# ScalarE in a written-out order beside TensorE, in the three attention stages of a two-layer decoder

## The chip, the cores and the metric

The kernel runs on one core of one Trainium2 chip, in one launch. The metric is the device time of that core in microseconds. It is built with a tile framework: the program says which engine runs each operation, the framework adds the semaphores, places the buffers of each named pool, and puts each engine's instructions in order. Inside a block called a manual schedule, the engines that are named keep the order in which the program states their operations; all others are ordered by the framework's planner, which uses costs of its own.

PE is TensorE, DVE is VectorE, ACT is ScalarE, POOL is GpSimd and SP is SyncE, whose queue issues most of the loads.

## The reference, cut to what matters

The input x has 16 sequences of 112 rows of 512 values. Two layers follow each other, each with a self attention, a cross attention and a feed-forward part:

```python
x = x + _L0_attn_ref(_layernorm(x), qkv, proj)       # 16 heads of 32, over the sequence axis
x = x + _L0_xattn_ref(_layernorm(x), ctx, ...)       # fp8-rounded inputs; self and cross attention
x = x + _L0_ffn_ref(_layernorm(x), ...)              # mixture of 8 experts
x = x + _L1_attn_ref(_layernorm(x), ...)             # 16 heads of 32, causal
x = x + _L1_xattn_ref(_layernorm(x), ctx, ...)
x = x + _L1_ffn_ref(_layernorm(x), ...)              # ternary weights
```

The change touches three of these: the two attentions with 16 heads of 32, and the self attention of the fp8 part:

```python
# _L0_attn_ref and _L1_attn_ref, per sequence and head
scores = q @ k.T * scale            # causal mask
probs  = softmax(scores)
out    = (probs @ v) @ w_proj.T

# _L0_xattn_ref, self part
ln  = _ln(x, ln_w, ln_b)
xq  = fp8(bf16(clip(ln / in_scale)))          # four scales: q, k, v and the cross part's q
q   = _ln(xq @ wq.T); k = _ln(xq @ wk.T); v = xq @ wv.T      # 16 and 8 heads of 128
core = softmax(q @ k.T / sqrt(128)) @ v
out  = fp8(core / smooth) @ wproj.T           # the self half of the projection
```

## The kernel before

The program runs seven stages in a row, each with its own buffers. Three of them put PE's order down by hand, in a manual schedule for PE alone.

**The two narrow attentions** (`stage_attn0`, `stage_attn1`, both through `narrow_attention`). The work is cut into quads: one quad is one group of 128 rows (first attention, 14 quads in blocks of 2, 4, 4, 2 and 2) or one sequence of 112 rows (second attention, 16 quads in blocks of 4), with 16 heads as four quarters of four heads. `NarrowQuad` has its steps:

- `scores`: four mask products (L168) and 16 score products in fp32 (L175) into one PSUM tile of four banks, of which there is one. Then, for each quarter, DVE takes the row maximum (L182) and scales it (L183), ACT takes four exponentials with their sums (L187), DVE the reciprocal (L191), and POOL multiplies (L192).
- `transpose_probs`: PE transposes a quarter's probabilities (L199) into the single buffer `tr`, and ACT copies it to SBUF (`ptt`, L201).
- `values`: PE multiplies with the values (`ps_av`, L208), and after the last quarter DVE copies the result (L213).

While quad n's scores are made, quad n-1 is transposed and multiplied quarter by quarter, quad n-2 gets its output product (`after`: `ps_o`, L273, and the sum onto x), and between the quarters the next block is prepared (`before`): the normalized input is transposed (`NormedRows.transpose`, L117, also through `tr`, with ACT's copy L149), the queries and keys are made as long products of four matmuls over 512, 448 or 256 columns (`wide`, L310 and L1199), and the values (L319, or L273). Each step carries a cost, and the loop spreads the steps over the quarters by it:

```python
for r in range(4):
    if n:
        made[n - 1].transpose_probs(r)
    while todo and used + todo[0][0] / 2 < budget * (r + 1) / 4:
        cost, step = todo.pop(0)
        used += cost
        step()
    if r == 1 and n > 1:
        quads[n - 2][0].after(quads[n - 2][1])
    if n:
        made[n - 1].values(r)
```

The first attention also gets the weights of the next stage ready (`Weights.part`): SP loads 512 columns, ACT scales them (L493), DVE takes the mean of each head away where the part is centred (L478 to L480), ACT writes the rounded half (L497) and POOL the rest (L498). Twelve such parts are asked for at once, as block 2 is prepared.

**The fp8 self attention** (`stage_fp8_self`). The four head groups of the 16 sequences are 64 units, and `turn(n)` works on five of them at once: unit n is projected (`ps_q` and `ps_kv`, L510, with the squares L589 and L591, the norm by POOL L408 and L409, the products L595 and the copy of v, L599), unit n-1 is transposed and scaled (L608, L400), unit n-2 gets scores and exponentials (L616, L622 to L625, L630), unit n-3 is transposed (L636, L638) and multiplied with its values (L644), then rounded to fp8 (`smooth_fp8`: L657, L421 to L426, whose result is `r_o`), and unit n-4 gets its output product (`ps_acc`, L510, added at L670). For the first head group a turn also takes the inputs of unit n+2: PE transposes them (L117), ACT scales them in 16 instructions (L538), and DVE and POOL round them. Turns also ask for two or three parts of coming weights.

The PSUM tags hold: `mm` two buffers in the narrow attentions and three in the fp8 stage, `tr` one, `sc` four, and in the narrow attentions four banks of scores and one of values.

Of the kernel before, what the change touches and what calls it, by code (L numbers as in the profile page):

```python
# [9 lines left out]
F32 = mybir.dt.float32  # L10
# [118 lines left out]
class NormedRows:  # L129
# [16 lines left out]
    def transpose(self, i):  # L146
        t = self.t
        ps = transposed(self.k, self.xn[i], t)
        self.k.nc.scalar.copy(self.xt[:, :, i * t : (i + 1) * t], ps)  # L149
        if i + 2 < len(self.rows):  # L150
            self.normalize(i + 2)


class NarrowQuad:
# [9 lines left out]
    def scores(self):  # L164
# [14 lines left out]
        self.pr = []  # L179
        for r in range(4):  # L180
            mx = k.small.tile([t, 4], F32, tag="nq_m", name="nq_m", bufs=6)
            nc.vector.tensor_reduce(mx, ps[:, :, r * t : (r + 1) * t], AX.X, ALU.max)  # L182
            nc.vector.tensor_scalar(mx, mx, -self.scale, None, ALU.mult)  # L183
            sums = k.small.tile([t, 4], F32, tag="nq_s", name="nq_s")
            pr = wk.tile([t, 4, t], F32, tag="pr", name="pr", bufs=8)
            for j in range(4):
                nc.scalar.activation(  # L187
                    pr[:, j, :], ps[:, j, r * t : (r + 1) * t], AF.Exp, bias=mx[:, j : j + 1],
                    scale=self.scale, accum_out=sums[:, j : j + 1],
                )  # L190
            nc.vector.reciprocal(sums, sums)  # L191
            nc.gpsimd.tensor_tensor(pr, pr, bc(sums.unsqueeze(2), [t, 4, t]), ALU.mult)  # L192
            self.pr.append(pr)
# [22 lines left out]
def narrow_attention(k, blocks):  # L216
# [5 lines left out]
    with k.tc.manual_schedule(engines={mybir.EngineType.PE}):  # L222
# [3 lines left out]
        for n in range(len(quads) + 1):  # L226
            budget = 0.0
            if n < len(quads):
# [4 lines left out]
                budget = sum(cost for cost, _ in todo) / (block.groups - group)  # L233
                made.append(block.quad(group))
                made[n].scores()
            used = 0.0
            for r in range(4):
                if n:
                    made[n - 1].transpose_probs(r)
                while todo and used + todo[0][0] / 2 < budget * (r + 1) / 4:  # L240
                    cost, step = todo.pop(0)
                    used += cost
                    step()
                if r == 1 and n > 1:
                    quads[n - 2][0].after(quads[n - 2][1])
                if n:
                    made[n - 1].values(r)
            while n < len(quads) and todo and group == block.groups - 1:
                todo.pop(0)[1]()
        block, group = quads[-1]  # L250
        block.after(group)
# [27 lines left out]
class Attn0Block:  # L279
# [13 lines left out]
    def before(self):  # L293
# [13 lines left out]
        def wide(dst, w):  # L307
            ps = k.psum.tile([P, 512], F32, tag="mm", name="ps_q", bufs=2)
            for c in range(KC):
                nc.tensor.matmul(ps[:, :n], w[:, c], xt[:, c, :n], start=c == 0, stop=c == 3)  # L310
            nc.vector.tensor_copy(dst, ps[:, :n])

        def queries(g):
# [1266 lines left out]
```

## Time and profile before

| | |
|---|---|
| median of 3 runs | 4186.39 us (4182.59, 4191.33, 4186.39) |
| profiled execution | 4182.83 us |
| its span | 4181.1 us |
| instructions | 47902 |
| PE busy | 3821.5 us, 91% |
| DVE busy | 1857.1 us, 44% |
| ACT busy | 1480.5 us, 35% |
| POOL busy | 946.0 us, 23% |
| mean granted clock of TensorE | 0.954 |

The span runs from the first to the last instruction; the execution's own time is 1.7 us longer. PE and PEld are the matmuls and the weight loads of TensorE. A group of the profile is named by its line, engine, operation and tiles, out first; a wait is named by the waiting instruction and by what ended its wait. Shares are averages over seven stages that differ, so stretches of the span are read one by one.

### The profile page before, as it was taken

Reading aid. Unit: us, or ns where it says so; the run is one execution under the profiler, and the core shown is the slowest. Engines: PE = TensorE matmul, PEld = TensorE weight load, DVE = VectorE, ACT = ScalarE, POOL = GpSimd, SP = SyncE. Lnnn points to the kernel's source line nnn. Section 1 sums busy time; section 2 is a strip of 40 time slices with the busy share of each in tenths; the row PEclk is TensorE's granted clock in tenths of the full one; section 3 lists DMA queues with packets and bytes.
Section 4 is the critical chain, followed back from the end, with each engine's and each line's share of the span. In section 5 each row is a group of like instructions: output and inputs, shape, how many; then the busy total and the mean of one; then the engine's idle time right before and its main releaser. Section 6 shows DMA issues by size and latency. Waiting matters only on the chain.

```text
span 4181.1 us, 47902 instructions
## 1 busy us (share of the span) xinstructions
PE 3821.5 (91%) x17118; PEld 2451.9 (59%) x17118; DVE 1857.1 (44%) x4310; ACT 1480.5 (35%) x4185; POOL 946.0 (23%) x1253
## 2 busy tenths in 40 slices
PE   6875887989999999999999999999988989999999
PEld 4444676777566566656666665444434445556887
DVE  4445666675544544554445533111243444214333
ACT  4446656554433433343333321111123341111222
POOL 3224445553322322232222210000122120000000
PEclk8987999999999999999999989999988989999999
DMA  2213212331211211111121113888830004112000
GB/s 84 54 46 120 84 71 99 120 124 69 76 49 48 76 41 48 58 54 48 48 76 46 48 34 124 290 297 295 286 129 11 1 1 130 68 59 90 10 9 18
DMA packets 99759, 359.95 MB, mean 86 GB/s; under 512 B 11952, under 2 KB 26288, under 8 KB 89936
## 3 DMA queue, kind: packets, MB, share of 16 engines
q1 hardware_dynamic: 86784, 327.47, 24.0%
q0 software_dynamic: 5360, 16.52, 1.1%
q10 hardware_dynamic: 7376, 12.89, 0.8%
q8 instruction: 135, 2.21, 0.2%
q14 instruction: 104, 0.85, 0.1%
HBM read 316.47 MB, written 40.37 MB: 85 GB/s over the span
## 4 chain that ended last, share of the span: by engine, by line
PE 70%; DVE 5%; ACT 3%; POOL 2%; DMA 2%; issue 1%; ACTq 0%; SPq 0%; DVEq 0%; POOLq 0%
PE ps_kv L788 14%; PE ps_o L273 5%; PE ps L1104 5%; PE ps_acc L510 4%; PE ps_s L815 3%; PE ps_av L838 3%; PE ps_q L510 3%; PE ps_y L1124 3%; PE ps_o L1391 3%; PE ps_pt L828 3%; PE ps_u L1409 3%; PE ps_q L1199 3%; PE ps_g L1409 2%; PE ps_p L1260 2%; PE ps L1076 2%; PE ps_o L1086 1%
## 5 line engine op out<-in xcount | busy, mean ns | idle before, releaser
L788 PE MATMUL ps_kv<-w_kv,ct 128*125 128x512 f32 x1536 | 690.1, 592 | 0.0
L788 PEld LDWEIGHTS ps_kv<-w_kv,ct 128*125 128x125 f32 x1536 | 287.6, 187 | 319.1 <-issue 278.8
L426 POOL TENSOR_TENSOR r_o<-r_t,r_m 128x448 fp32r<-128x448 bf16 x128 | 133.6, 1044 | 570.5 <-DVE r_t L425 538.8
L1104 PE MATMUL ps<-w_expert,xgt 128*128 128x448 f32 x560 | 219.6, 545 | 31.5 <-ACT xgt L1099 31.5
L409 POOL TENSOR_TENSOR cu_v<-cu_v,mhalf 125x2 f32<-125x2 f32 (+1 forms) x256 | 198.9, 777 | 21.2
L187 ACT ACTIVATE pr<-ps_s,nq_m 112x112 f32<-112x112 f32 (+1 forms) x480 | 166.3, 360 | 100.8 <-DVE nq_m L183 99.6
L192 POOL TENSOR_TENSOR pr<-pr,nq_s 112x448 f32<-112x448 f32 (+1 forms) x120 | 117.9, 982 | 367.7 <-DVE nq_s L191 341.3
L769 DVE TENSOR_REDUCE cu_v<-sq 125x2 f32<-125x256 f32 (+1 forms) x256 | 124.4, 486 | 163.2 <-ACT sq L768 163.2
L408 POOL TENSOR_SCALAR cu_v<-cu_v 125x2 f32<-125x2 f32 (+1 forms) x256 | 49.4, 193 | 650.4 <-DVE cu_v L769 641.2
L815 PE MATMUL ps_s<-kt,qt 128*112 128x375 f32 x512 | 184.0, 480 | 4.8 <-ACT pr L748 4.7
L1104 PEld LDWEIGHTS ps<-w_expert,xgt 128*128 128x128 f32 x560 | 103.6, 190 | 131.3 <-issue 87.7
L746 DVE TENSOR_REDUCE ex_m<-ps_s 112x1 f32<-112x375 f32 (+1 forms) x272 | 148.5, 546 | 62.3 <-PE ps_s L1284 60.2
L768 ACT ACTIVATE sq<-ps_kv 125x256 f32<-125x256 f32 x192 | 73.5, 383 | 268.7 <-PE ps_kv L788 222.2
L400 ACT ACTIVATE qt<-ps_t,vec 128x448 f32<-128x448 f32 x128 | 95.1, 743 | 207.1 <-PE ps_t L799 206.5
L748 ACT ACTIVATE pr<-ps_s,ex_m 112x375 f32<-112x375 f32 (+1 forms) x272 | 155.8, 582 | 28.3 <-DVE ex_m L747 28.3
L792 ACT COPY vn<-ps_kv 125x256 f32<-125x256 f32 x192 | 71.5, 372 | 264.6 <-DVE kn L771 264.6
L838 PE MATMUL ps_av<-pt,vn 125*128 125x224 f32 x768 | 158.7, 357 | 1.1 <-ACT pt L831 1.1
L510 PE MATMUL ps_acc<-w_cross,r_o 128*112 128x512 f32 x512 | 153.4, 422 | 3.2 <-POOL r_o L426 3.2
L838 PEld LDWEIGHTS ps_av<-pt,vn 125*128 125x128 f32 x768 | 147.1, 192 | 8.1 <-ACT pt L831 1.3
L815 PEld LDWEIGHTS ps_s<-kt,qt 128*112 128x112 f32 x512 | 89.5, 177 | 105.9 <-issue 45.7
L828 PEld LDWEIGHTS ps_pt<-ident,pr 112*125 112x125 f32 x768 | 107.8, 190 | 72.5 <-issue 29.0
L510 PE MATMUL ps_q<-w_cross,xq 128*112 128x512 f32 x512 | 150.1, 414 | 0.0
(279 smaller groups left out, 7726.3 us busy)
## 6 DMA issues: line engine op xcount, KB each, us to landing
w_expert<-in_moe_w SPq DMA_DIRECT2D x70, 896.0 KB
ct<-in_ctx_t SPq DMA_DIRECT2D x80, 750.0 KB
w_expert<-in_moe_w SPq DMA_DIRECT2D x35, 1024.0 KB
xq<-xq_dram SPq DMA_DIRECT2D x48, 672.0 KB
xq<-xx_dram SPq DMA_DIRECT2D x64, 224.0 KB
raw<-in_self_w SPq DMA_DIRECT2D x48, 256.0 KB
w_sum<-in_ffn_w SPq DMA_DIRECT2D x12, 1024.0 KB
cn<-in_ctx SPq DMA_DIRECT2D x16, 750.0 KB
```

The lines of the kernel that those rows point to most:

```text
L187: nc.scalar.activation(pr[:, j, :], ps[:, j, r * t : (r + 1) * t], AF.Exp, bias=mx[:, j : j + 1], scale=self.scale, accum_out=sums[:, j : ...
L273: k.nc.tensor.matmul(po, at[:, c, i * t : (i + 1) * t], w[:, c, :], start=c == 0, stop=c == nk - 1)
L409: nc.gpsimd.tensor_tensor(dst, dst, bc(k.minus_half[: dst.shape[0]], [dst.shape[0], n]), ALU.pow)
L510: k.nc.tensor.matmul(out, lhs(c), w[i][:, c, :], start=first and c == 0 and i == 0, stop=last and c == n - 1 and i == 1,)
L746: nc.vector.tensor_reduce(mx, src, AX.X, ALU.max)
L748: nc.scalar.activation(dst, src, AF.Exp, bias=mx, scale=scale, accum_out=sums)
L788: nc.tensor.matmul(pkv, self.ct[:, c, ch * CC : (ch + 1) * CC], w[:, c, :], start=c == 0, stop=c == 3)
L815: nc.tensor.matmul(ps, self.qt[:, h, :], self.kt[:, h // 2, :], start=True, stop=True)
L828: nc.tensor.transpose(ps[:, h, :], self.pr[:, h, ch * CC : (ch + 1) * CC], k.ident[:S, :S])
L838: nc.tensor.matmul(av[:, 2 * g : 2 * g + 2, :], self.vn[:, ch, g, :], self.pt[:, ch, 2 * g : 2 * g + 2, :], start=ch == 0, stop=ch == NCH - 1,
L1104: nc.tensor.matmul(pp, xt[:, c, :], w[:, c, :], start=c == 0, stop=c == 3)
L1409: nc.tensor.matmul(pp, w[:, c, cols], xt[:, part, c, :], start=c == 0 and part == 0, stop=c == 3 and part == 1,)
```

## The change

ACT joins PE in both manual schedules, so its instructions stand in the order of the program too. The program's order is changed to suit:

- In `NarrowQuad`, `scores` keeps the maxima of all four quarters, and the exponentials of a quarter become a step of their own, called after the copy of the same quarter of the quad before.
- The copy of the transposed input (L149) goes from ACT to DVE, in all three users of `NormedRows`: both narrow attentions and the cross attention of the second layer.
- Long products and output products are two steps of two matmuls each (`halves_of`); the steps of `after` stand in the middle of a quad's list.
- The parts of the next stage's weights are asked for one at a time, at the end of each quad (`aside`).
- In the fp8 stage the input's transposes open the turn, its 16 scalings are done as 5, 5 and 6, the projection is split in two with the squares behind each half and v's copy ahead of the norm, the exponentials follow the last scalings, and the values come last in the turn, after the output product.

```diff
-        self.k.nc.scalar.copy(self.xt[:, :, i * t : (i + 1) * t], ps)
+        self.k.nc.vector.tensor_copy(self.xt[:, :, i * t : (i + 1) * t], ps)
...
-        self.pr = []
+        self.ps, self.mx, self.pr = ps, [], []
         for r in range(4):
-            mx = k.small.tile([t, 4], F32, tag="nq_m", name="nq_m", bufs=6)
+            mx = k.small.tile([t, 4], F32, tag="nq_m", name="nq_m", bufs=8)
             nc.vector.tensor_reduce(mx, ps[:, :, r * t : (r + 1) * t], AX.X, ALU.max)
             nc.vector.tensor_scalar(mx, mx, -self.scale, None, ALU.mult)
...
+            self.mx.append(mx)
+
+    def exponentials(self, r):
...
+        for j in range(4):
+            nc.scalar.activation(
+                pr[:, j, :], self.ps[:, j, r * t : (r + 1) * t], AF.Exp,
+                bias=self.mx[r][:, j : j + 1], scale=self.scale, accum_out=sums[:, j : j + 1],
+            )
+        nc.vector.reciprocal(sums, sums)
+        nc.gpsimd.tensor_tensor(pr, pr, bc(sums.unsqueeze(2), [t, 4, t]), ALU.mult)
+        self.pr.append(pr)
...
+def halves_of(k, shape, tag, name, product, then):
+    got = []
+
+    def step(half):
+        if half == 0:
+            got.append(k.psum.tile(shape, F32, tag=tag, name=name, bufs=k.banks[tag]))
+        for c in range(half * KC // 2, (half + 1) * KC // 2):
+            product(got[0], c)
+        if half:
+            then(got[0])
+
+    return [lambda half=half: step(half) for half in range(2)]
...
-    with k.tc.manual_schedule(engines={mybir.EngineType.PE}):
+    with k.tc.manual_schedule(engines={mybir.EngineType.PE, mybir.EngineType.Activation}):
...
+            if n > 1:
+                after = quads[n - 2][0].after(quads[n - 2][1])
+                now[len(now) // 2 : len(now) // 2] = after
+            total, used = sum(cost for cost, _ in now), 0.0
             for r in range(4):
                 if n:
                     made[n - 1].transpose_probs(r)
-                while todo and used + todo[0][0] / 2 < budget * (r + 1) / 4:
-                    cost, step = todo.pop(0)
-                    used += cost
-                    step()
-                if r == 1 and n > 1:
-                    quads[n - 2][0].after(quads[n - 2][1])
+                if n <= last:
+                    made[n].exponentials(r)
+                while now and used + now[0][0] / 2 < total * (r + 1) / 4 + 1.0:
+                    used += now[0][0]
+                    now.pop(0)[1]()
                 if n:
                     made[n - 1].values(r)
...
+            if aside:
+                aside()
...
-        steps = blocks[2].before
-        blocks[2].before = lambda: k.next_w[0].step(12) and steps()
-        narrow_attention(k, blocks)
+        narrow_attention(k, blocks, lambda: k.next_w[0].step(1))
...
         def turn(n):
+            new = inputs.get(n + 2)
+            if new:
+                new.transpose()
+                new.scale(5)
             if at(n):
-                units[n].project(weights[order[n][0]], xq.pop(n))
+                units[n].project_q(weights[order[n][0]], xq.pop(n))
+            if new:
+                new.scale(5)
+            if at(n):
+                units[n].project_kv()
             if at(n - 3):
                 units[n - 3].transpose_probs()
             if at(n - 1):
                 units[n - 1].transpose()
+            if at(n - 2):
+                units[n - 2].scores()
+            if new:
+                new.scale(6)
+            if at(n - 2):
+                units[n - 2].exponentials()
+            if at(n - 4):
+                units[n - 4].output()
             if at(n - 3):
                 units[n - 3].values()
-            if at(n - 2):
-                units[n - 2].scores()
-            if at(n - 4):
-                units[n - 4].output()
-            if n + 2 in inputs:
-                inputs[n + 2].scaled()
-                xq[n + 2] = inputs[n + 2].rounded()
+            if new:
+                xq[n + 2] = new.rounded()
...
-        with k.tc.manual_schedule(engines={mybir.EngineType.PE}):
+        with k.tc.manual_schedule(engines={mybir.EngineType.PE, mybir.EngineType.Activation}):
             for n in range(-2, total):
                 turn(n)
```

## The prediction, made before the changed kernel ran

> **What bounds the kernel now.** I read the busy time by stage first, because the change touches three stages of seven: the first attention (0 to 335 us), the fp8 self attention (335 to 1045) and the second narrow attention (3095 to 3475). The columns are stretch and length, then busy us and instruction count of PE, PEld, DVE, ACT and POOL, the granted clock, and DMA.
>
> ```profile
> 0.00:335.00 335.00, 247.47 (x1656) 143.22 (x1656) 145.70 (x331) 140.60 (x561) 89.96 (x116) 0.85 0.23 63
> 335.00:1045.00 710.00, 587.93 (x3512) 498.77 (x3512) 471.69 (x1100) 411.91 (x1252) 343.20 (x348) 0.93 0.29 99
> 3095.00:3475.00 380.00, 331.92 (x1934) 166.26 (x1934) 145.54 (x330) 133.11 (x596) 84.57 (x89) 0.89 0.03 9
> ```
>
> PE is idle for 88, 122 and 48 us there, 258 of the 360 us that it is idle in the span, and its clock is granted at 0.85 to 0.93. No other engine is full: ACT has 42%, 58% and 35%. So order, not work, is the limit. Second, the waits (waiting instruction, releaser: us, times, longest), first attention and then fp8 stage:
>
> ```profile
> PE ps_av L208 <- ACT ptt L201: 35.9, 28, 4.6
> PE ps_xt L117 <- ACT xt L149: 14.8, 8, 5.9
> ```
> ```profile
> ACT v L599 <- DVE qk L595: 115.7, 58, 4.2
> PE ps_av L644 <- ACT pt L638: 49.4, 21, 4.0
> PE ps_pt L636 <- POOL pr L630: 40.1, 26, 3.4
> ```
>
> PE waits for copies that stand in ACT's queue behind something else. Third, the timeline of one turn of the first attention says behind what:
>
> ```profile
> 209.73 0.37 ACT L187 ACTIVATE pr<-ps_s,nq_m 128x128 f32<-128x128 f32 x1 [1.04 <-DVE nq_m L183]
> ...
> 211.27 0.18 DVE L191 RECIPROCAL nq_s<-nq_s 128x4 f32<-128x4 f32 x1 [1.31 <-ACT pr L187]
> 211.37 0.66 DVE L182 TENSOR_REDUCE nq_m<-ps_s 128x4 f32<-128x512 f32 x1
> ...
> 212.06 0.60 DVE L183 TENSOR_SCALAR nq_m<-nq_m 128x4 f32<-128x4 f32 x1
> ...
> 212.75 0.37 ACT L187 ACTIVATE pr<-ps_s,nq_m 128x128 f32<-128x128 f32 x1 [1.51 <-DVE nq_m L183]
> ...
> 214.13 0.59 ACT L201 COPY ptt<-ps_pt 128x512 f32<-128x512 f32 x1
> ...
> 214.78 0.66 PE L208 MATMUL ps_av<-ptt,vn 128*32 128x128 f32 x8 [4.56 <-ACT ptt L201]
> ```
>
> The reader is to see a loop between two engines: exponentials, reciprocal, next maximum, next exponentials. It turns in 3.02 us (209.73 to 212.75), of which ACT works 1.4, and three groups of exponentials pass before the copy that PE wants. In the fp8 stage 16 scalings are one block ahead of such a copy:
>
> ```profile
> 626.80 5.49 ACT L538 ACTIVATE y<-ps_xt,q_bias,q_gain 128x112 bf16<-128x112 f32 x16
> ...
> 633.53 1.02 PE L644 MATMUL ps_av<-pt,v 112*128 112x224 f32 x4 [2.72 <-ACT pt L638]
> ```
>
> **What the Trainium skill says.** "TensorE: Matmul & The Clock Gate", Part 1, says the array clock is throttled by default and released after about 3.4 us of sustained work. The trace agrees: eight matmuls of ps_o (L273) take 3.60 us between busy neighbours and 6.10 at 94.47, after waits. So a wait removed pays again in clock. "GPSIMD Engine Reference", section 8, says GpSimd shares its SBUF interfaces with VectorE. It fits L183, which takes 0.15 to 0.17 us alone and 0.60 while the 1.04 us product L192 runs on POOL. "Perfetto Trace Analysis", Sequencer Loop, describes an engine's instructions read in turn, each waiting for its semaphores; the 115.7 us that ACT stands before v (L599) is such a queue blocked at its head.
>
> **Part by part: the two attentions.** No arithmetic is added. In the built order of the changed kernel DVE takes the four maxima of a quad right after the scores, and ACT's order is copy, four exponentials, copy, and so on. The loop of 3.02 us becomes ACT's own work: copy 0.59 and exponentials 1.38 (206.72 to 208.10), 1.97 per quarter. A quad with nothing else on PE is then scores 2.07 (106.98 to 109.05), about 1.6 to the first maximum and its scaling, 4 x 1.97: 11.5, with handoffs 12 us. Any other quad is set by PE. Its pieces, start to start at full clock: scores 2.07; per quarter transposes 0.50 and values 0.36; a long product of 512 columns 3.43 to 3.53, of 256 columns 1.73; a value product 0.92; an input transpose 0.50. Halving the long products adds no matmul; it lets copy and exponentials pass beside each half of 1.75.
>
> What is late next is the input transposes: their copy goes from ACT to DVE (no row shows it; the like-sized copy L213 takes 0.69 against 0.59 on ACT), behind four maxima, through a single buffer. I add 6 us for every four transposes, 3 for two; it could be 2 to 10.
>
> First attention, against the starts of the mask matmuls (L168). Quads 2 to 5 take 86.9 now (78.95 to 165.80); PE needs 4 x (2.07 + 3.44 + 3.53) = 36.2, preparation 4 x 0.50 + 5 x 3.43 + 4 x 0.92 = 22.8, and 6: 65, so -22. Quads 6 to 9: 69.4 now; 36.2 + 11.5 + 3 = 51, -19. Quads 10 and 11: 38.4; 18.1 + 11.5 + 3 = 33, -6. Quads 12 and 13: 29.9; 24, -6. Quads 0 and 1: 53.3; 19.5 + 18 = 37.5, -16. Sum **-69**. The weights' loads move from one burst to one part after each quad: 12 loads on SP, 24 instructions on ACT and 6 centerings on DVE. On ACT a centred part is 0.72, some 1.9 for DVE (0.68 + 0.16 + 0.69 of L478 to L480, and handoffs) and 0.62; it lies after a quad's last exponentials, beside 2.07 of scores and 1.6 of maximum, so I cost it nothing. Without that cover it is 3.2 x 6 = 19 us. On SP they queue ahead of loads and stores that have a quad of slack.
>
> Second attention, scores 1.88, quarters 0.76: a block of four quads needs 4 x (1.88 + 3.04 + 3.53) + 1.7 + 24.8 + 14.1 = 74.4, with transposes 80. It takes 87.0 and 86.4 now (3218.09, 3305.11, 3391.48): -6.6, -6. The first four save 6 likewise. The last four have no preparation: 4 x 12 = 48 against 64.5, -16.5. Sum **-35**.
>
> I take three quarters of both, since each floor leaves out handoffs and DVE's order: -52 and -26.
>
> **The fp8 stage.** A turn of PE alone is 8.41 us (951.27 to 1010.14, equal turns). While inputs are scaled, turns average 11.3 (432.48 to 647.73, 19 turns). The change splits the 16 scalings into 5, 5 and 6, puts v's copy ahead of the qk product, so the 115.7 us of blocked ACT go, and puts the values last in the turn. Their copy then has 3.8 us in front of PE's use (0.74 + 0.95 + 2.08 of transposes, scores and output). The store of y follows the last scalings as before; an input's load has one turn ahead of its first use, not nearly two, against 2.9 to 5.9 us that the chain of waits shows for loads of r_y in this stage. ACT's sum in a turn with an input is 5.49 + 0.6 + 0.4 + 0.4 + 0.5 + 0.7 + 0.5 + 1.4 = 10.0, in one without 4.5; a pair is 14.5 against PE's 17.3, so it fits. I put the pair at 18.8: 19 turns save 36, of which I take 27. Against it: the transposes of input 2 now stand ahead of the first projection, which waits for a second block of 5.5 us: +5. And ACT waits in its order for each centring of weights, which the old order filled with other work: 22 centred parts at about 2 us, in turns with 3.6 us of free ACT. I count +12. Without any cover it is +44. Net **-10** (from -31 to +40).
>
> Elsewhere the copy L149 moves to DVE in the stage after (16 x 0.6 us), beside a PE that is busy 341 of 350 us (3470 to 3820): nothing, or 10 us if DVE is late. Untouched stages I leave at zero, within 5 either way.
>
> **The sum.** -52 - 26 - 10 = -88. The profiled execution takes 4182.83 (span 4181.1), so 4094.8; the median of the three runs is 3.56 above it: **4098 us**.
>
> **Rivals.** *A, the order of ACT eats the fp8 part.* For it: 22 centrings without cover and a DVE at 66% in that stage. Against it: the free 3.6 us. The fp8 stage then loses 25 instead of gaining 10: 4186 - 78 + 25 = 4133. *B, slower: the values at the end of the turn make the output wait.* Now a value product has some 10 us until the output reads its rounded result. Afterwards it is 5.9 (projections 3.8, transposes and scores 2.1). In DVE's built order the rounding stands behind the reciprocal, so behind the exponentials; in a turn with an input these end about 2.0 after the values, then 0.3 + 1.84 on DVE + 1.05 on POOL (L426) + 0.3: 5.5. The margin is 0.4. From there every us that ACT is late is a us of PE, in 64 turns; at 1.7 us late it is +109 and the sum +31: 4217. Against it: half the turns have no input, with 2 us more margin. *C, the quads stay paced:* exponentials now also wait for PE's transposes; if a quarter still takes 3 us, only the last quads and some fp8 turns gain, and the result is within 8 us: 4180.
>
> **How the numbers follow.** Forecast 0.71, A 0.15, B 0.10, C 0.04 (about half of C's width counted as no change). Faster by over 0.2%, which is 8.4 us and about what a measurement of this kernel can tell from no change: 0.86; within it 0.04; slower 0.10. Low end: all of the floors and a fp8 stage of -31, so 4186 - 135 = 4051; high end: half of the attentions' floors and +30, so 4164. Range 4050 to 4165.
>
> **What would show it.** Right: in the attentions the wait of PE ps_av for ptt near zero, exponential groups evenly 2 to 4 us apart, clock above 0.92; first attention near 283 us, second near 354. In the fp8 stage L538 in groups of 5 and 6, no wait of ACT v for qk, ps_av waiting little. Wrong: a new wait of PE ps_acc for POOL r_o (B), ACT w_self waiting for DVE raw for over 40 us (A), or quads with no preparation still above 15 us (C).

## The result, and the profile after

The changed kernel takes **4146.44 us** (median of 4 runs, 4141.81 to 4151.72), against 4185.09 for the kernel before (4 runs): a ratio of 0.9906, 95% interval 0.9889 to 0.9923. The change gains 39 us where 88 were forecast. The profiled execution has a span of 4142.4 us and a mean granted clock of 0.959. Below, "before" and "after" are the two kernels of this case.

The busy time by stage of after, in the same columns as before: the first attention, the fp8 self attention and the second narrow attention.

```profile
0.00:292.00 292.00, 229.15 (x1660) 131.75 (x1660) 136.38 (x346) 133.53 (x557) 91.23 (x116) 0.92 0.29 75
292.00:1030.00 738.00, 579.30 (x3513) 495.41 (x3514) 489.56 (x1101) 400.45 (x1243) 346.04 (x348) 0.91 0.29 94
3088.00:3440.00 352.00, 321.08 (x1932) 159.05 (x1932) 139.92 (x347) 122.63 (x577) 81.15 (x86) 0.94 0.05 14
```

In the two attentions PE's idle time is down and its clock is up, 0.85 to 0.92 and 0.89 to 0.94. In the fp8 stage the work is the same, the stretch is longer, and the clock has fallen from 0.93 to 0.91. Three points in the timelines measure this. The first fp8 projection starts at 301.69 us, not 344.81: **-43.1**. From it to the first cross projection the stage takes 729.8 us, not 702.2: **+27.6**. The second attention, from its first input transposes to the next stage's first projection, takes 353.6 us, not 381.7: **-28.1**. The stages that the change hardly touches make up the remaining +4.9.

The waits of after in the fp8 stage (waiting instruction, releaser: us, times, longest) name the new holder. The first attention's old wait comes last:

```profile
PE ps_acc L544 <- ACT pt L692: 64.5, 18, 10.6
ACT w_self L531 <- DVE raw L514: 45.2, 18, 5.1
PE ps_acc L544 <- POOL r_o L460: 13.7, 24, 3.3
ACT w_cross L531 <- DVE raw L514: 15.4, 4, 6.8
```
```profile
PE ps_av L212 <- ACT ptt L205: 7.5, 8, 1.6
```

ACT's wait before v is gone from the list, and PE's wait for ptt has fallen from 35.9 to 7.5 us. In their place ACT waits 60.6 us for the centring of weight parts (45.2 + 15.4), and PE waits 64.5 us for pt at its output product. The timeline of one turn shows how the first makes the second:

```profile
581.26 0.36 ACT L679 ACTIVATE pr<-ps_s,su_m 112x112 f32<-112x112 f32 x1
581.58 0.73 ACT L527 ACTIVATE raw<-raw,w_cols 128x512 f32<-128x512 f32 x1
...
583.27 0.55 PE L690 MATMUL ps_pt<-ident,pr 112*112 112x112 f32 x4
...
584.22 0.62 ACT L531 CAST w_self<-raw 128x512 fp32r<-128x512 f32 x1 [1.91 <-DVE raw L514]
...
584.75 0.72 ACT L527 ACTIVATE raw<-raw,w_cols 128x512 f32<-128x512 f32 x1
...
587.98 0.62 ACT L531 CAST w_self<-raw 128x512 fp32r<-128x512 f32 x1 [2.51 <-DVE raw L514]
...
589.94 0.72 ACT L527 ACTIVATE raw<-raw,w_cols 128x512 f32<-128x512 f32 x1 [1.34 <-POOL w_self L532]
...
592.46 0.62 ACT L531 CAST w_self<-raw 128x512 fp32r<-128x512 f32 x1 [1.80 <-DVE raw L514]
592.99 0.59 ACT L619 ACTIVATE sq<-ps_q 112x512 f32<-112x512 f32 x1
...
593.99 0.56 ACT L692 COPY pt<-ps_pt 112x448 f32<-112x448 f32 x1
...
594.69 3.72 PE L544 MATMUL ps_acc<-w_self,r_o 128*112 128x512 f32 x8 [9.51 <-ACT pt L692]
```

The probabilities are transposed at 583.27, some 0.6 us of PE work. Their copy pt is written behind three weight parts. Each part is a scaling, a wait for DVE, and a cast; the third scaling also waits until a raw buffer is free and loaded, because there are two. So the copy comes at 593.99, and PE, which needs its PSUM bank, stands for 9.51 us.

### The profile page after: what moved, and what is told of

It reads as the page before. It is cut to its first block, busy times and chain, and to the rows that moved or that the text cites. A ratio compares the mean times of both kernels' runs of the same rounds, so it can differ in the third digit from the quotient of the medians.

```text
span 4142.4 us, 47854 instructions
## 1 busy us (share of the span) xinstructions
PE 3783.4 (91%) x17118; PEld 2434.7 (59%) x17118; DVE 1866.1 (45%) x4356; ACT 1445.5 (35%) x4139; POOL 950.3 (23%) x1253
## 4 chain that ended last, share of the span: by engine, by line
PE 70%; DVE 9%; ACT 4%; POOL 4%; issue 2%; DMA 2%; ACTq 0%; POOLq 0%; DVEq 0%
PE ps_kv L853 15%; PE ps L1169 5%; PE ps_acc L544 4%; PE ps_s L880 4%; PE ps_av L903 3%; PE ps_q L544 3%; PE ps_y L1189 3%; PE ps_o L1476 3%; PE ps_o L303 3%; PE ps_pt L893 3%; PE ps_u L1494 3%; PE ps_q L1263 2%; PE ps_g L1494 2%; PE ps_p L1345 2%; PE ps L1141 2%
## 5 line engine op out<-in xcount | busy, mean ns | idle before, releaser
L853 PEld LDWEIGHTS ps_kv<-w_kv,ct 128*125 128x125 f32 x1536 | 287.8, 187 | 318.8 <-issue 278.7
L460 POOL TENSOR_TENSOR r_o<-r_t,r_m 128x448 fp32r<-128x448 bf16 x128 | 134.1, 1048 | 448.7 <-DVE r_t L459 395.0
L544 PE MATMUL ps_acc<-w_self,r_o 128*112 128x512 f32 x512 | 153.2, 447 | 81.9 <-ACT pt L692 64.5
L544 PEld LDWEIGHTS ps_acc<-w_self,r_o 128*112 128x112 f32 x512 | 95.6, 198 | 116.5 <-POOL w_self L532 40.1
L857 ACT COPY vn<-ps_kv 125x256 f32<-125x256 f32 x192 | 71.5, 372 | 264.8 <-DVE kn L836 264.8
L836 DVE TENSOR_TENSOR kn<-ps_kv,cu_v 125x256 f32<-125x256 f32 x192 | 81.6, 425 | 153.9 <-POOL cu_v L443 153.9
```

The source lines that it names most:

```text
L460: nc.gpsimd.tensor_tensor(dst, t, m, ALU.subtract)
L544: k.nc.tensor.matmul(out, lhs(c), w[i][:, c, :], start=first and c == 0 and i == 0, stop=last and c == n - 1 and i == 1,)
L853: nc.tensor.matmul(pkv, self.ct[:, c, ch * CC : (ch + 1) * CC], w[:, c, :], start=c == 0, stop=c == 3)
```

## The experiments

In all of them the fp8 stage is measured from first to first: unit n's projection starts turn n. The turns up to 23 take in the inputs of the first head group; turns 0 to 5 get ready the weight parts of group 1, turns 26 to 38 get ready most of the weight parts of groups 2 and 3; turns 36 to 51 also quantise the cross inputs (`quantize_cross`); turns 48 to 54 get the parts of the cross stage. The column "stage" runs from the first projection to the first cross projection, so it holds turn 63 and the end of the stage too. All times are us, read from the timelines, one profiled execution each. A ratio compares with runs of before from the same session; in brackets is its 95% interval. Eight kernels of this document have the fp8 program of new_pe_vals: their stages measure 661.4 to 671.0, and their single columns agree within 2.1.

| kernel | 0-8 | 8-26 | 26-38 | 38-48 | 48-54 | 54-63 | stage |
|---|---|---|---|---|---|---|---|
| before | 103.0 | 199.9 | 129.1 | 93.5 | 64.1 | 75.7 | 702.2 |
| after | 101.0 | 176.7 | 150.5 | 104.9 | 78.5 | 76.7 | 729.8 |
| attn_only | 102.2 | 203.2 | 131.1 | 90.5 | 65.1 | 75.5 | 704.5 |
| new_pe | 88.7 | 177.1 | 134.8 | 104.3 | 70.7 | 77.3 | 690.8 |
| nocenter | 86.9 | 176.8 | 134.5 | 105.3 | 71.5 | 76.8 | 689.8 |
| spread | 98.2 | 176.7 | 132.9 | 105.1 | 75.9 | 76.3 | 703.6 |
| noround | 101.1 | 176.6 | 150.5 | 86.9 | 70.4 | 76.7 | 702.3 |
| new_pe_vals | 88.2 | 179.1 | 130.4 | 91.0 | 64.4 | 76.9 | 669.5 |
| fixed_vals | 106.2 | 175.7 | 164.1 | 90.9 | 77.1 | 77.0 | 728.4 |
| inputs_last | 100.2 | 206.6 | 130.4 | 90.2 | 64.0 | 76.9 | 706.7 |
| best_spread | 89.2 | 177.2 | 130.7 | 88.4 | 67.8 | 76.9 | 669.7 |

### Order held by whom: ScalarE, or the turn

The first question is which half of the stage's change costs: that ACT is fixed, or that the turn has a new order. Two edits, alone and together, make three kernels beside after.

**attn_only**: `Quantized`, `SelfUnit` and `stage_fp8_self` as before, so the fp8 part of the diff above is undone line by line.

> The two narrow attentions as after, the fp8 self stage as before (its turn order, ScalarE left to the scheduler). Theory (the whole loss is in the fp8 stage, and the stages don't act on each other): first self projection to first cross projection back from 729.8 to about 702 us, total 4146 - 28 = 4118 us. Rival (part of the loss comes from what the new attention hands on: weight parts of group 0 spread over the quads, a later DMA tail): the stage stays above 712 us and the total above 4128.

Measured: 4116.17 us, ratio 0.983 (0.9814 to 0.9846); stage 704.5. The loss lies in the fp8 stage: with that stage's program as before, the attentions keep their gain and the stage is back at before's time.

**new_pe**:

```diff
-        with k.tc.manual_schedule(engines={mybir.EngineType.PE, mybir.EngineType.Activation}):
+        with k.tc.manual_schedule(engines={mybir.EngineType.PE}):
             for n in range(-2, total):
                 turn(n)
```

> The kernel after, with ScalarE of the fp8 stage left to the scheduler; the turn's new order stays, for TensorE. Theory (the fixed ScalarE order costs in the weights and the quantising turns): turns 26-38, 38-48 and 48-54 go back to about 129, 94 and 64 us, and turns 8-26 keep part of their gain, stage 680 to 705 us, total 4097 to 4121. Rival (the turn's order costs): those turns stay at 150, 105 and 78 us, total about 4146.

Measured: 4109.62 us, ratio 0.9817 (0.9801 to 0.9834); stage 690.8. The theory holds for the weights turns (150.5 to 134.8, 78.5 to 70.7) and turns 0-8 (101.0 to 88.7), and falls for turns 38-48, which stay at 104.3: they aren't long because ACT is fixed.

**old_act**: attn_only, with the same line the other way:

```diff
-        with k.tc.manual_schedule(engines={mybir.EngineType.PE}):
+        with k.tc.manual_schedule(engines={mybir.EngineType.PE, mybir.EngineType.Activation}):
             for n in range(-2, total):
                 turn(n)        # before's turn
```

> As the kernel attn_only, but ScalarE too follows the written order in the fp8 stage, with the turn's order of before (projection whole, maxima and exponentials together, the 16 scalings at the turn's end, values ahead of scores). Theory (a fixed ScalarE order is what costs): the weights turns 26-38 and 48-54 stay at about 150 and 78 us or above, the stage at 730 us or more, total 4146 or more. Rival (the new order of the turn costs, whoever holds to it): these turns go back to about 129 and 64 us, total near 4118.

Measured: 4443.34 us, ratio 1.0624 (1.0606 to 1.0642). It is far worse than either theory said. Its waits from 400 to 700 us, in which PE is busy for only 195 us:

```profile
PE ps_av L678 <- ACT pt L672: 111.9, 19, 10.5
ACT v L633 <- DVE qk L629: 80.2, 19, 5.1
```

In before's turn v's copy is stated after the qk product. Held to that, ACT stands there in every turn, and pt's copy behind it. So the new turn, taken whole, isn't what costs in after: it is what makes a fixed ACT bearable at all. One step of it does cost, as the runs below show.

### What holds ScalarE in the weights turns

**nocenter**: after, with the centring of the parts of groups 1 to 3 and of the cross queries left out. It computes something else, and serves to price the centring.

```diff
-        if centered:
+        if centered and self.means:    # False for the weights made in this stage
             self.center(k, raw)
```

> The kernel after, with the centring of the weight parts of groups 1 to 3 and of the cross queries left out in the fp8 self stage; scalings, casts and low parts stay in their places. Theory (the casts' waits for centring hold ScalarE): turns 26-38 from 150.5 us to about 132, turns 48-54 from 78.5 to about 72. Rival (the wait for the second pair of raw buffers and their transfer holds it, 2.5 us for every third part): 26-38 stay above 142 us.

Measured: 4109.65 us (one run); stage 689.8, which is 40.0 less than after and within 1 us of new_pe. Its wait of PE for pt at the output product:

```profile
PE ps_acc L544 <- ACT pt L692: 38.4, 17, 5.2
```

It falls from 64.5, and the waits for centring are gone; turns 26-38 and 48-54 are where the theory had them. Turns 0-8, with group 1's parts, fall to 86.9. The raw buffers, the rival, are not needed to explain the difference. Nor is the centring's own work on DVE, all of which new_pe still does.

**spread**: after, with one part after the key and value projection, one after the scores and one at the turn's end, and each cast at the next of these places.

```diff
-        nc.scalar.copy(hi, raw)
-        nc.gpsimd.tensor_tensor(lo, raw, hi.bitcast(F32), ALU.subtract)
+        def cast():
+            nc.scalar.copy(hi, raw)
+            nc.gpsimd.tensor_tensor(lo, raw, hi.bitcast(F32), ALU.subtract)
+
+        self.late.append(cast)          # done ahead of the next part, or at the next place
```

> The kernel after, with the weight parts of groups 2, 3 and of the cross stage spread over the turn: one part's scaling after the key/value projection, one after the scores, one at the turn's end, and each part's cast only at the next of these places, so that its centring has time. Theory (the casts that wait for centring, and the third scaling that waits for its raw buffer, hold the copy of the probabilities behind them on ScalarE): turns 26-38 and 48-54 fall from 150.5 and 78.5 us to about 130 and 65, total 4146 - 34 = 4112. Rival (the weights turns are long because VectorE or GpSimd carry more work there, whatever ScalarE's order): less than 10 us off them, total above 4136.

Measured: 4120.95 us, ratio 0.9848 (0.9832 to 0.9865); turns 26-38 take 132.9. The same parts with the same centring cost 17.6 us less there, in other places of the same fixed order. In turns 48-54 only 2.6 us came back, so the expected 34 us became 25.

### What makes the quantising turns long

Two units' rounding chains stand on DVE in these turns. After's timeline shows the loop that they are links of; "<-" in brackets is what ended the idle time ahead:

```profile
786.38 0.59 DVE L711 TENSOR_TENSOR r_y<-ps_av,r_smooth 128x448 bf16<-128x448 f32 x1
...
788.32 0.39 DVE L459 TENSOR_TENSOR r_t<-r_y,r_m 128x448 bf16<-128x448 bf16 x1
...
788.82 0.68 DVE L620 TENSOR_REDUCE su_v<-sq 112x4 f32<-112x512 f32 x1
...
790.85 1.04 POOL L460 TENSOR_TENSOR xqx<-r_t,r_m 128x448 f32<-128x448 bf16 x1 [0.95 <-DVE r_t L459]
...
793.49 0.69 DVE L646 TENSOR_TENSOR qk<-ps_q,su_v 112x512 f32<-112x512 f32 x1 [2.39 <-POOL su_v L443]
...
794.43 0.61 DVE L671 TENSOR_REDUCE su_m<-ps_s 112x4 f32<-112x448 f32 x1
...
795.37 0.36 ACT L679 ACTIVATE pr<-ps_s,su_m 112x112 f32<-112x112 f32 x1 [5.55 <-DVE su_m L672]
```

The exponentials wait for the maxima, the maxima stand on DVE behind the next unit's qk, qk waits for the power on POOL, the power for the reduction of the squares, and the reduction stands on DVE behind the values' rounding (786.38 to 788.7). The squares stand on ACT behind the exponentials. The loop turns in 10.57 us (784.80 to 795.37).

**noround**: after, with the rounding of the cross inputs left out, to price it.

```diff
-    round_fp8(k, wk, y, xq)
+    k.nc.vector.tensor_copy(xq, y)
```

> The kernel after, with the rounding of the cross inputs in turns 36-51 left out: one VectorE copy in place of four VectorE operations and GpSimd's subtraction. Theory (VectorE's four operations and GpSimd's 1.04 us are links of the loop): turns 38-48 from 104.9 us to TensorE's own pace of about 86 us. Rival (ScalarE's order makes these turns long): above 98 us.

Measured: 4122.82 us (one run); turns 38-48 take 86.9, near TensorE's own pace (ten turns of 8.41 us). So what makes them long is the rounding's work on DVE and POOL, and not ACT's order.

**new_pe_vals**: new_pe, with the values ahead of the scores as in before.

```diff
+            if at(n - 3):
+                units[n - 3].values()
             if at(n - 2):
                 units[n - 2].scores()
...
             if at(n - 4):
                 units[n - 4].output()
-            if at(n - 3):
-                units[n - 3].values()
```

> The kernel new_pe with the values of a unit back at their old place in the turn, ahead of the next unit's scores. Theory (at the turn's end the values' rounding, 2.2 us of VectorE, falls into the loop maxima - exponentials - squares - reduction - power - queries and keys - maxima): turns 38-48 fall from 104.3 us to 88-94, total about 4110 - 12 = 4098. Rival (the quantising turns are long because of the exponentials' place behind the scalings, or because of the quantising alone): they stay above 100 us, total 4110 or, if the input turns lose what they gained, 4125-4135.

Measured: **4081.85 us**, ratio 0.9747 (0.9730 to 0.9763); stage 669.5, turns 38-48 91.0. This is the best version found. The same place in its timeline:

```profile
732.80 0.69 DVE L646 TENSOR_TENSOR qk<-ps_q,su_v 112x512 f32<-112x512 f32 x1 [1.79 <-POOL su_v L443]
733.41 0.41 DVE L646 TENSOR_TENSOR qk<-ps_kv,su_v 112x256 f32<-112x256 f32 x1
733.74 0.61 DVE L711 TENSOR_TENSOR r_y<-ps_av,r_smooth 128x448 bf16<-128x448 f32 x1
...
735.26 0.35 ACT L679 ACTIVATE pr<-ps_s,su_m 112x112 f32<-112x112 f32 x1 [3.46 <-DVE su_m L672]
...
735.73 0.39 DVE L459 TENSOR_TENSOR r_t<-r_y,r_m 128x448 bf16<-128x448 bf16 x1
```

The values' rounding now lies ahead of the exponentials and beside them, not between them and the next reduction, and the exponentials' wait falls from 5.55 to 3.46 us. In new_pe, where ACT is free as well, it is still 5.55 to 5.57 us in nine of these turns, so it is the values' move that shortens it.

**fixed_vals**: the same move of the values, with the same diff, in after.

> The kernel after, ScalarE fixed as it stands, with the values alone back ahead of the next scores. Theory (two separate losses: ScalarE's order in the weights turns, the values' place in the quantising turns): turns 38-48 fall from 104.9 to about 91 us, turns 8-26 stay near 177, turns 0-8 and 26-38 stay near 101 and 148; total 4146 - 22 = 4124. Rival (the two act on each other: with the values early TensorE meets the held-up copy of the probabilities one step sooner, so the weights turns grow): total above 4140.

Measured: 4142.10 us, ratio 0.9899 (0.9883 to 0.9916), which can't be told from after. The rival was right: turns 38-48 fall to 90.9, but turns 26-38 grow to 164.1. The wait for pt only changed its place in PE's order, from the output product to the values:

```profile
PE ps_av L698 <- ACT pt L692: 101.1, 44, 9.2
ACT w_self L531 <- DVE raw L514: 38.5, 18, 5.1
```

So the two losses overlap. The values' late place costs 21.3 us while ACT is free (new_pe against new_pe_vals) and nothing that can be measured while it is fixed (after against fixed_vals). That late values need pt's copy later fits this, but was not tested apart. A fixed ACT costs 39.0 us with the values late and 58.9 with them early.

**best_spread**: new_pe_vals with the diff of spread.

> The kernel new_pe_vals with the weight parts spread over the turn and each cast put off to the next place. Theory (the weights turns' remaining excess over 8.5 us each is still the parts' chain of scaling, centring and cast): turns 26-38 fall from 130.4 us to 115-122, total 4082 - 10 = 4072. Rival (with ScalarE left to the scheduler the parts no longer hold the path; the excess is the uncovered inputs of the next group and VectorE's work): 26-38 stay at 128-134 us, total 4078-4088.

Measured: 4084.37 us, ratio 0.976 (0.9744 to 0.9776), turns 26-38 130.7: the rival. What is left in these turns over TensorE's 8.4 us each is not the parts' place.

### Where the gain of the input turns comes from

**inputs_last**: new_pe_vals with

```diff
-            if new:
-                new.transpose()
-                new.scale(5)
...
-            if new:
-                new.scale(5)
...
-            if new:
-                new.scale(6)
...
             if new:
+                new.transpose()
+                new.scale(16)
                 xq[n + 2] = new.rounded()
```

> The kernel new_pe_vals with the input's transposes and its 16 scalings in one piece at the end of the turn, as before; all else stays. Theory (their place at the head of the turn gives the gain in turns 8-26): these turns go from 179.1 us back to about 200, total 4082 + 22 = 4104. Rival (the gain comes from the split projection or from the exponentials' and the output's places): they stay below 185 us.

Measured: 4120.40 us (one run); turns 8-26 at 206.6, turns 0-8 at 100.2, stage 706.7. The place of the inputs gives 37.2 us, 27.5 of them in turns 8-26. It also has a price that falls ahead of the stage as measured here. A third block of transposes now stands before the first projection and waits for 16 scalings; in after:

```profile
301.01 1.01 PE L117 MATMUL ps_xt<-ident,xn 112*128 112x112 f32 x4 [5.62 <-ACT y L577]
```

From the first input transposes to the first projection after takes 13.9 us, before and inputs_last 7.8 and 7.7. The net gain is 31 us.

### The attentions

The first two columns are the distance from the first to the last quad's mask product (14 quads in the first attention, 16 in the second), which the expectations use. It leaves out the last quad's own chain and the end of the attention. So the other two run on from the first mask product to the next stage's first matmul.

| kernel | first | second | first, to next stage | second, to next stage |
|---|---|---|---|---|
| before | 262.5 | 297.0 | 311.3 | 330.2 |
| after | 217.4 | 274.2 | 260.9 | 300.8 |
| new_pe_vals | 217.1 | 274.4 | 260.8 | 301.0 |
| nine others with after's attentions | 218.9 to 220.4 | 274.3 to 275.0 | 263.1 to 265.5 | 300.6 to 301.8 |
| all_pe: ScalarE free | 224.3 | 272.2 | 270.2 | 297.4 |
| maxima_late: maxima where the exponentials are | 221.3 | 278.8 | 270.1 | 306.7 |
| whole: products in one step | 223.4 | 278.0 | 273.3 | 308.4 |
| maxima_free: late maxima, ScalarE free | 226.1 | 279.4 | 273.2 | 307.2 |
| old_quads: all three | 235.3 | 282.8 | 287.1 | 317.9 |
| old_burst: and the weight parts in a burst | 242.0 | 279.7 | 295.0 | 313.0 |
| xt_act, best: input copies on ScalarE | 220.4, 220.5 | 278.7, 278.8 | 263.8, 263.8 | 305.3, 305.5 |

Eleven kernels, after and new_pe_vals among them, have the same attentions. In the first they differ by 3.3 us in the first column and by 4.7 in the third, so a smaller difference there shows nothing. A price given as a range, "5 to 9", is against all eleven.

**all_pe**: new_pe with the same edit in `narrow_attention`:

```diff
-    with k.tc.manual_schedule(engines={mybir.EngineType.PE, mybir.EngineType.Activation}):
+    with k.tc.manual_schedule(engines={mybir.EngineType.PE}):
         for _, step in blocks[0].before():
```

> The kernel new_pe with ScalarE left to the scheduler in the narrow attentions as well: every other part of the change stays. Theory (the quads gain by maxima ahead of the exponentials and by the halves, ScalarE's fixed order adds little): the first fp8 projection starts within 5 us of 306.6 and the second attention takes within 5 us of after's, total about 4110. Rival (ScalarE's fixed order is what paces the quads): 20 to 60 us of the attentions' 70 are lost, total 4130 to 4170.

Measured: 4113.04 us, ratio 0.9826 (0.9809 to 0.9842), not distinguishable from new_pe (220.0 and 274.3 in this measure). Against new_pe a fixed ACT gives 4 us in the first attention and takes 2 in the second, 5 and 3 up to the next stage.

**maxima_late**: new_pe_vals, with the loop of maxima back.

```diff
-        for r in range(4):
-            mx = k.small.tile([t, 4], F32, tag="nq_m", name="nq_m", bufs=8)
...
     def exponentials(self, r):
+        mx = k.small.tile([t, 4], F32, tag="nq_m", name="nq_m", bufs=8)
+        nc.vector.tensor_reduce(mx, self.ps[:, :, r * t : (r + 1) * t], AX.X, ALU.max)
+        nc.vector.tensor_scalar(mx, mx, -self.scale, None, ALU.mult)
```

> The kernel new_pe_vals with each row's maxima and their scaling taken where its four exponentials are issued, as before, in both attentions; halves and ScalarE's fixed order stay. Theory (the maxima ahead of the exponentials turn a loop of 3.0 us for each row into ScalarE's own 2.0): the first fp8 projection moves from 301 to 335-345 us, the second attention's 16 quads get slower by 15 to 27 us, total about 4130 to 4150. Rival (the halves, which let the transposed probabilities through between two pieces of a product, give the gain): the first fp8 projection stays before 315 us.

Measured: 4091.61 us (one run), first fp8 projection at 311.12. From first to last mask the second attention loses 4 us, and the first 1 to 4, which is hardly over the spread; up to the next stage it is 5 to 6 and 5 to 9. That is far from the theory, though ACT's timeline shows that the loop is back:

```profile
148.24 0.37 ACT L189 ACTIVATE pr<-ps_s,nq_m 128x128 f32<-128x128 f32 x1 [0.21 <-DVE nq_m L185]
...
150.11 0.59 ACT L203 COPY ptt<-ps_pt 128x512 f32<-128x512 f32 x1 [0.36 <-PE ps_pt L201]
151.37 0.37 ACT L189 ACTIVATE pr<-ps_s,nq_m 128x128 f32<-128x128 f32 x1 [0.67 <-DVE nq_m L185]
```

Its first exponentials are 3.13 us apart, the copy between them. Four times 3.1 is less than the 15 us or more that a quad with preparation takes, so there the loop doesn't decide. In the first attention the first interval is even shorter with it, 19.2 us against 21.8 to 22.3. The loop decides in quads with little or no preparation: the second attention's last three intervals are 13.4, 17.1 and 17.1 us before, 13.5, 16.1 and 15.0 here, and 11.9, 12.8 and 11.9 after.

**whole**, **maxima_free** and **old_quads**, each from new_pe_vals: the first with one step in place of two, the second with the edits of maxima_late and all_pe, the third with all of these and the exponentials called in `scores`.

```diff
-    return [lambda half=half: step(half) for half in range(2)]
+    def whole():
+        step(0)
+        step(1)
+
+    return [whole]        # at the cost of both
```

> The kernel new_pe_vals with the long products, values and output products of the narrow attentions whole again, four matmuls in one step. In new_pe_vals the mask products of the 14 quads lie 217.1 us apart from the first to the last, those of the 16 quads 274.4 us (before: 262.5 and 297.0). Theory (the halves let copies and exponentials pass beside each piece of 1.75 us, and are the main gain): 235 to 255 and 282 to 295. Rival (the halves add little where ScalarE's order is fixed, since a whole piece of 3.5 us still fits between copy and values): below 222 and 279.

> The kernel maxima_late with ScalarE of the attentions left to the scheduler. Alone, the late maxima made the quads' distances 221.3 and 278.8 us, and the free ScalarE 224.3 and 272.2. Theory (the fixed order and the early maxima stand in for each other: either keeps three groups of exponentials from passing ahead of a copy): 240 us or more and 285 or more. Rival (neither matters): below 229 and 284.

> The kernel new_pe_vals with the quads' core as before: maxima and exponentials together with the scores, ScalarE left to the scheduler, whole products. What stays of the change in the attentions: the input copies on VectorE, the weight parts one for each quad, and the spreading of the steps over the quarters. Theory (halves, maxima and fixed order together are the gain): the quads' distances go back to within 8 us of 262.5 and 297.0, total near 4082 + 60. Rival (the input copies on VectorE and the spreading are a good part): 245 or below, and 288 or below.

Measured (one run each): 4092.51, 4091.16 and 4121.03 us. The halves are worth 6.3 and 3.6 us against new_pe_vals: over the rival's bound in the first attention, under it in the second. Late maxima with a free ACT cost 9.0 and 5.0: they don't stand in for each other. All three together cost 18.2 and 8.4, within the bounds of old_quads' rival. But that measure flatters: up to the next stage they cost 22 to 26 us of a gain of 46 to 51, and 16 to 17 of 28 to 30. The totals agree with this: old_quads takes 39 us more than new_pe_vals. So the three edits together make about half of the attentions' gain.

**old_burst**, from old_quads, **and xt_act and best**, from new_pe_vals:

```diff
-        narrow_attention(k, blocks, lambda: k.next_w[0].step(1))
+        steps = blocks[2].before
+        blocks[2].before = lambda: k.next_w[0].step(12) and steps()
+        narrow_attention(k, blocks)
```
```diff
-        self.k.nc.vector.tensor_copy(self.xt[:, :, i * t : (i + 1) * t], ps)
+        self.k.nc.scalar.copy(self.xt[:, :, i * t : (i + 1) * t], ps)
```

> The kernel old_quads with the twelve weight parts of the next stage asked for in one burst as block 2 is prepared, as before. Theory (the steps' new places, with transposes, halves of products and the output in one list over four quarters, make old_quads' gain in both attentions): the distance of the 14 quads stays within 6 us of 235.3. Rival (in the first attention it is the burst's 12 scalings, centrings and casts among the copies): 250 us or more.

> The kernel new_pe_vals with the copies of the transposed inputs back on ScalarE, in its fixed order. The prediction charged their move to VectorE with 6 us for four transposes, some 18 us in the first attention and 24 us in the second. If that was right, the quads' distances shrink by about that, to 200-210 and 250-262 us; if the copies on ScalarE stand behind exponentials, they grow, by 5 us or more; if neither, they stay within 4 us of 217.1 and 274.4.

> The kernel xt_act again, timed: after's attentions with the input copies on ScalarE, the fp8 stage's new turn with ScalarE left to the scheduler and the values at their old place. If xt_act's single time holds, 4075 us; new_pe_vals had 4081.9. If its 7 us came from the stages that it does not change, 4080 to 4083.

Measured: old_burst 4130.24 us (one run), so spreading the weight parts is worth 6.7 us in the first attention (7.9 up to the next stage), just past the theory's bound. Up to the next stage 16.3 us of the gain in the first attention and 17.2 in the second stay with the steps' new places and the input copies. xt_act took 4075.26 us in its one run, but best, the same kernel, 4086.19 (5 runs, 4081.63 to 4086.47), ratio 0.9761 (0.9748 to 0.9775): no better than new_pe_vals. The 7 us weren't repeated; where they came from is open.

## Where the prediction failed, and where it held

**The fp8 stage's term failed: -10 forecast, +27.6 measured.** Another 6.1 us, which the forecast booked in this term as +5, fall ahead of the first projection. A chain of kernels takes the stage apart: before 702.2, inputs_last 706.7, new_pe_vals 669.5, new_pe 690.8, after 729.8. From before to inputs_last everything else of the new turn changes at once, for 4.5 us, within the spread of kernels with equal programs; each later step changes one thing.

- *Inputs.* The prediction put the input turns at -36 and took -27. The step measured -37.2. Mechanism and size were right, and the discount was not needed; the +5 for input 2's transposes came in at 6.1.
- *Centring.* This is the mis-sized term: +12 was counted, with +44 "without any cover". It measured 40.0 (after against nocenter). The 22 parts do wait about 2 us each, but the "turns with 3.6 us of free ACT" were no cover. A spare total in a turn helps only if the spare stands behind the wait; here the squares, v and pt stood behind it in the queue, and PE behind pt. The working also priced each wait alone, where three parts stand in one turn and the third waits for its buffer as well.
- *Values last.* The sum had nothing for it. Rival B asked only whether PE would wait for r_o, and that wait is 13.7 us. The cost was on the other side: the rounding moved from beside the exponentials into DVE's queue ahead of the next reduction, 21.3 us while ACT is free. `quantize_cross` was not in the working at all, and in its turns that loop becomes the bound.

**Rival A was the nearest.** Its sign, ACT w_self waiting for raw over 40 us, came in at 45.2, its stage at +27.6 for +25 forecast; it was given 0.15. That the sum came so near is in part luck: it too had nothing for the values' 21.3 us, and the input turns gave 10 us more than it counted. Its total of 4133 missed by 13 us: the attentions gave 71 and not 78, and the stages outside the three lost 4.9.

**The attentions' terms held in size, and for their reason only in part.** -52 and -26 were forecast, -43.1 and -28.1 measured. The -43.1 is a sum: the quads gave 45.1 us, the last quad and the end of the attention 5.3; against them stand the 6.1 of the input's transposes, which the forecast had booked in the fp8 term, and a first quad 1.2 us later. So the attention alone gave 50.4 up to the next stage, close to the 52. At its end the wait for the first input's load grew by 4.1 us, from 13.8 to 17.9; it is 17.7 to 18.1 in every kernel with the new steps, and why is open. The clock rose as the prediction had it.

But the loop of 3.02 us, named as the pace of the attentions, is worth 5 to 9 us in the first and 5 to 6 in the second up to the next stage. Maxima, fixed order and halves together make about half of the gain. About 16 and 17 us stay when these and the spread weight parts are put back: they belong to the steps' new places, with the output in one list with the rest, and to the input copies on VectorE. Which of the places does it was not tried further. The charge for VectorE's input copies, 6 us for every four transposes, was wrong: with the copies back on ScalarE the first attention can't be told from the others, and the second takes 4 us more, not less.

## What to carry to other kernels

Fixing an engine's order turns each of its waits into a wait of everything stated after it: before doing so, list for each instruction that waits for another engine what stands behind it, and price it in full unless the consumer of that queue has slack at that very place. Look for the cost of a moved step on the engines that it uses, not only at the reader of its result: a loop through several in-order queues can close in a turn that carries extra work. And try the new order without the fixing: here, with ScalarE left to the planner in the fp8 stage, it gave 77 us in place of 39, and 103 with the values back at their old place.

## What the runs showed of the hardware

A short VectorE operation can be stretched by a GpSimd operation beside it by more than the prediction's 0.17 to 0.60 us. In after's weights turn, the scaling of four means (L513) takes 0.16 us with GpSimd idle and 0.94 beside its subtraction L532:

```profile
583.14 0.16 DVE L513 TENSOR_SCALAR w_mean<-w_mean 128x4 f32<-128x4 f32 x1
...
585.87 1.26 POOL L532 TENSOR_TENSOR w_self<-raw,w_self 128x512 fp32r<-128x512 f32 x1
...
586.22 0.94 DVE L513 TENSOR_SCALAR w_mean<-w_mean 128x4 f32<-128x4 f32 x1
```

It ends with the subtraction, at 587.1, and the cast behind this centring waits 2.51 us, where the other two of the turn wait 1.91 and 1.80. The rest of after's trace shows the same. The 40 times that L513 runs with no GpSimd operation beside it, it takes 0.15 to 0.17 us; 13 of the other 16 take 0.23 to 1.61, and each of these ends 0.02 to 0.03 us after a GpSimd operation. In new_pe_vals the bf16 clipping L455 takes 0.96 us at 736.48, beside GpSimd's L460, and 0.27 at 734.80. Not every operation is open to this: the reduction L512 of 512 columns keeps its 0.65 to 0.69 us beside GpSimd in after.
